# A transformer block's MLP on one core: at the change of layers, three hidden sums are issued ahead of the last additions, and these go from VectorE to GpSimd with their gelus spread over the next products

## The chip, the cores and the metric

The kernel runs on one core of a Trainium2 chip. A core has TensorE (PE, matrix products into PSUM), VectorE (DVE), ScalarE (ACT), GpSimd (POOL) and SyncE (SP, which here only issues DMA transfers). Each engine works through its own queue in order and waits on semaphores that the others raise. The metric is the device time of one execution in microseconds (us). A profiled execution gives the span, from the first to the last instruction.

## The reference

The input x has 2 sequences of 2048 tokens with 512 features, all float32. A condition vector per sequence is turned into shifts, scales and gates. Cut to what matters:

```python
mod = silu(condition) @ Wada + bada
sh_a, sc_a, gt_a, sh_m, sc_m, gt_m = split(mod, 6)
xm = layernorm(x) * (1 + sc_a) + sh_a
x = x + gt_a * attention(xm, Wqkv, Wproj, bproj)      # causal, 16 heads of 32
xm = layernorm(x) * (1 + sc_m) + sh_m
h = gelu(xm @ W1 + b1)                                # 512 -> 2048
x = x + gt_m * (h @ W2 + b2)                          # 2048 -> 512
```

The change touches the last two lines.

## The kernel before, in words

The first two thirds of the span are the projections and the attention of the two sequences; the MLP starts at about 1519 us. It runs over four blocks m = 0 to 3 of 1024 tokens each. In a block, the first layer makes the hidden values h, and the second layer (`tail`) makes the output.

Both layers use Strassen's scheme in Winograd's form: a product of 2x2 blocks is made with seven block products instead of eight, named A11, S1, A12, S2, S3, A22, S4, at the price of sums of blocks of weights and tokens before, and of additions of results after. In blocks 1 to 3 both layers do it on two levels: seven outer products, each of seven inner ones.

*First layer, blocks 1 to 3* (`pair_of_sets`, p = 0 to 3). Pair p makes the hidden features of two columns of 128 in both halves, as four results d00, d01, d10, d11 (d with half and token group), each of two tiles of 128x512. Three phases issue the seven outer products, two or three side by side; `phase` issues in each of seven rounds one inner product of each of its outer products on PE, and behind it the evictions: a copy by ACT (L2162, L2174) or an addition by DVE (`combine`, L1728). Additions between results (`add`, L2221) go to POOL. The last phase makes A22 onto d10 and S3 into t3 (two tiles: in pairs 2 and 3 those of the buffer `Y`, y in the profile's names). Then t3 is added to d11 and to d10, two instructions of 128x512 each. With that the pair's hidden values are whole, and four gelus (L2214, one for each tile of d11 and d10) follow on ACT. In pairs 0 to 2 the additions are POOL's, and the gelus are put on a list (`self.later`) that the next pair's first phase issues after its rounds 3 to 6. In the last pair (`final`) the additions are DVE's, and the four gelus are issued at once, ahead of all of the second layer.

*Second layer* (`tail`). It calls `hid.outer` seven times, in the order A11, S1, A12, S2, S3, A22, S4 of the outer products. Each `outer` calls `seven`, which issues seven products on PE in the order A11, S1, S2, S4, S3, A12, A22 (four matmuls of 128x256 each, which the profile shows as eight instructions) into three PSUM banks a, b and c: A11, S2, S3 and A22 go to a, one on top of the other, S1 and S4 to b, A12 to c. After each, the bank is read before the next product goes on top: in the first outer product, A11, S1 and S2 are copied by ACT into spare tiles (c, L2317), S4, S3 and A12 are combined by DVE into y (L1728), and A22 is copied by ACT into y (L2327).

*Hidden sums* (`Hidden`). The second layer's products need sums of blocks of h. They stand in one list in a fixed order (`todo`): A11's first; the first two of T1 (a difference of whole blocks); S1's first; A11's second, third and fourth; the last two of T1; S1's second to fourth; and so on. A sum (`difference`, L1631) is one instruction of 128x1024. A11's first, T1's first two and S1's first are POOL's, the others DVE's. `pop` issues the next one, if a buffer is free for it. In the last pair's phases the first four are popped, after round 3 of the second phase and after rounds 0, 2 and 4 of the third. In `tail`, `then(k)` pops one after each product k = 0 to 6. `need` is called ahead of a product and pops as many as that product requires: ahead of S1 in the first outer product A11's first and second, ahead of S2 the second and fourth (and so the third).

What else runs beside the tail in blocks 0 to 2: the next block's tokens are loaded (L2452), normalised by ACT (L1622, issued after the fourth product of each of the first four outer products), transposed by PE (ps_xt) after the seventh, and modulated by ACT (L275). The sums for the next block's first layer (L1793, most by POOL) come at the tail's end.

*Order.* The order of each queue is that in which the Python program issues: `act`, `mm` and the helpers around them keep program order. Weights are loaded by SP into four buffers (L1661, L1668); `next_weights` issues the next load when a set has been used. A load waits for its buffer.

Of the kernel before, what the change touches and what calls it, by code (L numbers as in the profile page):

```python
# [27 lines left out]
def dit_block_kernel(  # L28
# [36 lines left out]
    nc = tc.nc  # L65
# [1528 lines left out]
    with ExitStack() as mlp:  # L1594
# [246 lines left out]
        class Hidden:  # L1841
# [3 lines left out]
            def __init__(self):  # L1845
                self.h = [
                    [
                        mp.tile([P, C, MT], F32, tag="h4", name="h4", bufs=2 * FC // C)
                        for _ in range(FC // C)
                    ]  # L1850
                    for _ in range(2)
                ]
                self.todo, self.made, self.at = [], set(), 0
                self.slots, self.later, self.flip = {}, {}, False
                self.t = {n: {} for n in OUTER}
                x = {
                    (g, half): {
                        (j, t): self.h[g][2 * half + j][:, :, t * half_t : (t + 1) * half_t]
                        for j in range(2)
                        for t in range(2)  # L1860
                    }
                    for g in range(2)
                    for half in range(2)
                }
                t1 = {}
                b11, b12, b21, b22 = x[0, 0], x[1, 0], x[0, 1], x[1, 1]
                self.x = {
                    A11: b11, S1: t1, A12: b21, S2: b11, S3: b12, A22: b21, S4: b22,
                }

                def difference_of(name, dst, u, v, after, js=range(2)):
                    for j in js:
                        for t in range(2):
                            self.task(
                                (name, j, t),
                                lambda j=j, t=t: difference(dst[j, t], u[j, t], v[j, t]),
                                after,
                            )

                def first_sums(j):  # L1880
                    for t in range(2):
                        def run(t=t):
                            t1[j, t] = self.take()
                            engine = nc.vector if j else nc.gpsimd
                            difference(t1[j, t], b12[j, t], b11[j, t], engine)
                        self.task(("T1", j, t), run, takes=True)

                def inner(n, ks=(1, 2, 3, 4)):
                    for k in ks:
                        self.task((n, k), lambda k=k: self.inner_sum(n, k), takes=True)  # L1890

                inner(A11, (1,))
                first_sums(0)
                inner(S1, (1,))
                inner(A11, (2, 3, 4))
                first_sums(1)
                inner(S1, (2, 3, 4))
                inner(A12)
                difference_of("T2", b11, b22, t1, 1)
                self.task(("T1", "done"), lambda: self.give(*t1.values()), 2)  # L1900
                inner(S2)
                difference_of("T3", b12, b22, b12, 0)
                inner(S3)
                difference_of("T4", b21, b21, b11, 3)
                inner(A22)
                inner(S4)
# [291 lines left out]
            def pair_of_sets(self, p, among):  # L2198

                final = p == HF // 2 - 1  # L2200
                fs = (2 * p, 2 * p + 1)

                def part(half, g):
                    return [self.part(half, g, f) for f in fs]

                d00, d01, d10, d11 = (part(h, g) for h in range(2) for g in range(2))
                if p < 2:
                    t3 = [self.part(1, 1, f + HF // 2) for f in fs]
                else:
                    t3 = [Y[p][:, j] for j in range(2)]  # L2210

                def gelu(half, d, j):
                    act(
                        nc.scalar.activation(  # L2214
                            d[j], d[j], AF.Gelu, bias=col(r_b1 + half * HF + fs[j], 1)
                        )
                    )

                def add(engine, d, x):
                    for j in range(2):  # L2220
                        act(engine.tensor_tensor(d[j], d[j], x[j], ALU.add))  # L2221

                def phase(ph, jobs):
                    self.flip = not self.flip
                    lanes = []
                    for o, job in enumerate(jobs):
                        if o < 2:
                            banks = bank_pair(self.flip)
                        else:
                            banks = [  # L2230
                                ps_mm.tile(
                                    [P, MT], F32, tag="aa", name=f"ps_{n}", bufs=2
                                )[:, :half_t]
                                for n in "ab"
                            ]
                        n, *to = job
                        lanes.append(self.two_level(n, self.set_of(p * 7 + n), banks, *to))
                    for r in range(7):
                        for lane in lanes:
                            lane[r]()  # L2240
                        among(ph, r)
                        if r in self.later.get(ph, ()):
                            for f in self.later[ph].pop(r):
                                f()
                    for n, *_ in jobs:
                        q = p * 7 + n
                        if q % 2 or q == HF // 2 * 7 - 1:
                            next_weights()
                        if final:
                            sums.append(xi.pop(n))  # L2250
                            k = {S1: 1, S2: 2, S3: 3, A22: 4}.get(n)
                            if k:
                                sums.append(sx.pop(k))

                phase(0, ((S1, d11), (S2, d10), (A11, d00)))
                add(nc.gpsimd, d10, d00)
                add(nc.gpsimd, d11, d10)
                phase(1, ((S4, d01), (A12, d00, d00)))
                add(nc.gpsimd, d01, d11)
                self.later[2] = {  # L2260
                    0: [lambda: gelu(0, d00, 0)], 1: [lambda: gelu(0, d00, 1)],
                    4: [lambda: gelu(0, d01, 0)], 6: [lambda: gelu(0, d01, 1)],
                }
                phase(2, ((A22, d10, d10), (S3, t3)))
                add(nc.vector if final else nc.gpsimd, d11, t3)
                add(nc.vector if final else nc.gpsimd, d10, t3)
                ends = [
                    lambda d=d, j=j: gelu(1, d, j) for d in (d11, d10) for j in range(2)
                ]
                if final:  # L2270
                    for f in ends:
                        f()
                else:
                    self.later[0] = {r: [f] for r, f in enumerate(ends, 3)}

# [69 lines left out]
        def tail(m, hid, among, each):  # L2345

            u, c22, c11, c12 = Y
            later = []

            def gate(y, half):
                later.extend(lambda i=i: gated(m, y, half, i) for i in range(2))

            for n, dst, base in (
                (A11, u, None),  # L2360
                (S1, c22, None),
                (A12, c11, u),
                (S2, u, u),
                (S3, u, u),
                (A22, u, u),
                (S4, c12, c12),
            ):

                def then(k):
                    if k in (1, 3) and later:  # L2370
                        later.pop(0)()
                    hid.pop()
                    among(n, k)

                hid.outer(n, dst, base, then, each if n == S4 else None)
                if n == A12:
                    gate(c11, 0)
                elif n == S2:
                    combine(c12, u, c22)
                elif n == S3:  # L2380
                    combine(c22, c22, u)
                    gate(c22, 1)
                elif n == A22:
                    gate(u, 1)
                elif n == S4 and not each:
                    gate(c12, 0)
            for f in later:
                f()
# [137 lines left out]
```

## Time and profile before

| | |
|---|---|
| median of 3 runs | 2253.81 us (2253.27 to 2258.36) |
| the profiled execution | 2258.55 us, span 2256.8 us |
| PE busy | 2202.7 us, 98% of the span |
| DVE / POOL / ACT busy | 1577.0 / 1429.7 / 1038.1 us |
| the additions L2221 on DVE | 12 in all, four in each of blocks 1, 2 and 3 |
| the four additions in blocks 1, 2 and 3 | start 1787.65, 1970.12 and 2153.51 us, 6.1 us together each time |

A row of the timeline gives the start and the duration in us, the engine, the line, the operation, the tile written, an arrow and the tiles read, the shapes, the number of instructions that the row merges, and in brackets how long the engine sat idle before it and what ended that. PE's ends are modelled, so the time between two products is read from their starts. A row of the windows view gives a stretch, its length, the busy time of PE, PEld (weight loads), DVE, ACT and POOL with the number of instructions, the granted clock of PE (1.00 is full), the share of the DMA engines and GB/s.

### The profile page before, as it was taken

To read this page: it belongs to the slowest core of one execution; us is meant where nothing else is said; L and a number is where in the kernel's file an instruction comes from. 1 tells how busy PE (TensorE), PEld (TensorE's weight loads), DVE (VectorE), ACT (ScalarE), POOL (GpSimd) and SP (SyncE) were. 2 spreads that over 40 slices of the span, in tenths; PEclk is the share of its full clock that TensorE was granted. 3 is DMA by queue.
4 is the path that set the end of the run, shared out by engine and by line. 5 is a ranking of instruction groups with operands and counts; after the bars stand their busy time and mean duration, and the time that the engine had idled before them with its cause. 6 is when DMAs were issued, how large, how long until landed. Compare 5 with 4: busy or idle time off the path is not lost.

```text
span 2256.8 us, 34324 instructions
## 1 busy us (share of the span) xinstructions
PE 2202.7 (98%) x12273; PEld 1475.6 (65%) x12273; DVE 1577.0 (70%) x3385; ACT 1038.1 (46%) x2132; POOL 1429.7 (63%) x891
## 2 busy tenths in 40 slices
PE   7999999999999999999999999999999999999998
PEld 5887555555543588755555555345788888888887
DVE  4678767777757667777677766664686686677576
ACT  4434555655564243355656556513324423532510
POOL 4253998998983695299989898448417516605520
PEclk9999999999999999999999999999999999999999
DMA  8787142231324799533324123367656455554543
GB/s 271 247 277 192 43 93 70 62 85 48 107 95 147 241 308 312 157 77 74 73 75 95 48 60 133 107 228 262 212 167 213 146 178 180 189 163 159 191 149 108
DMA packets 166627, 340.99 MB, mean 151 GB/s; under 512 B 17216, under 2 KB 49516, under 8 KB 164664
## 3 DMA queue, kind: packets, MB, share of 16 engines
q1 hardware_dynamic: 158080, 302.05, 44.0%
q0 software_dynamic: 8000, 36.21, 4.3%
q8 instruction: 97, 1.59, 0.3%
q14 instruction: 74, 0.61, 0.1%
q10 hardware_dynamic: 376, 0.55, 0.1%
HBM read 246.46 MB, written 100.14 MB: 154 GB/s over the span
## 4 chain that ended last, share of the span: by engine, by line
PE 87%; DVE 6%; POOL 3%; DMA 2%; ACT 1%; issue 1%; SPq 0%; DVEq 0%; ACTq 0%; POOLq 0%
PE ps_a L207 23%; PE st L207 18%; PE ps_b L207 13%; PE o L207 10%; PE s L207 9%; PE ps_c L207 4%; PE sm L207 3%; PE ps_o L207 2%; DVE junk L499 1%; POOL ee L696 1%; PE ps_xt L215 1%; ACT e L671 1%; DVE mx L505 1%; DVE h L2221 1%; PE ps_o L215 1%
## 5 line engine op out<-in xcount | busy, mean ns | idle before, releaser
L671 ACT ACTIVATE e<-st 128x512 f32<-128x512 f32 (+1 forms) x1152 | 574.8, 578 | 362.4 <-PE st L207 313.6
L505 DVE TENSOR_REDUCE mx<-s 128x1 f32<-128x512 f32 x576 | 381.8, 686 | 193.8 <-PE s L207 192.8
L696 POOL TENSOR_TENSOR ee<-ee,e 128x2048 f32<-128x2048 f32 x106 | 485.9, 4584 | 10.3 <-ACT e L671 4.4
L207 PE MATMUL st<-qst,kst 128*128 128x512 f32 (+3 forms) x1280 | 408.6, 386 | 0.0
L207 PE MATMUL s<-kst,qst 128*128 128x512 f32 (+3 forms) x1046 | 380.6, 395 | 5.7 <-DVE mx L505 3.7
L207 PE MATMUL ps_a<-sum,w 128*128 128x256 f32 (+1 forms) x1304 | 340.9, 396 | 12.3 <-DVE sum L1631 11.7
L207 PE MATMUL o<-e,vv 128*32 128x512 f32 (+3 forms) x2560 | 293.2, 537 | 0.3 <-POOL e L683 0.3
L207 PEld LDWEIGHTS st<-qst,kst 128*128 128x128 f32 x1280 | 228.5, 188 | 97.7 <-issue 65.9
L207 PEld LDWEIGHTS ps_a<-sum,w 128*128 128x128 f32 x1304 | 249.2, 193 | 55.3 <-ACT c L2317 12.8
L499 DVE CUSTOM_DVE_ANT_0 junk<-s,causal 128x128 bf16<-128x128 f32 (+3 forms) x470 | 220.7, 470 | 61.0 <-PE s L207 47.0
L207 PEld LDWEIGHTS s<-kst,qst 128*128 128x128 f32 x1046 | 194.8, 188 | 70.7 <-DVE mx L505 17.0
L696 POOL TENSOR_TENSOR ee<-e 128x2048 f32<-128x2048 f32 x42 | 192.5, 4584 | 42.6 <-ACT e L671 42.6
L207 PE MATMUL ps_b<-sum,w 128*128 128x256 f32 (+1 forms) x744 | 186.5, 381 | 0.0
L2221 POOL TENSOR_TENSOR h<-h,h 128x512 f32<-128x512 f32 x96 | 119.3, 1273 | 69.6 <-DVE h L1728 69.6
L207 PEld LDWEIGHTS <-sel 32*128 32x128 bf16 x1152 | 29.5, 91 | 197.0 <-issue 196.1
L207 PEld LDWEIGHTS ps_b<-sum,w 128*128 128x128 f32 x744 | 140.7, 190 | 21.7 <-issue 2.6
L1793 POOL TENSOR_TENSOR sum<-xm 128x256 f32<-128x256 f32 x22 | 23.1, 1052 | 185.4 <-PE ps_a L207 185.4
L505 DVE TENSOR_REDUCE mx<-st 128x1 f32<-128x512 f32 x192 | 131.1, 683 | 0.5
L683 POOL TENSOR_SCALAR_AFFINE_SELECT e<-e 128x512 f32<-128x512 f32 x128 | 83.3, 669 | 67.4 <-ACT e L671 67.3
L207 PEld LDWEIGHTS o<-e,vv 128*32 128x32 f32 x2560 | 59.1, 108 | 92.4 <-issue 73.3
L207 PE MATMUL st<-fold,sel 32*128 32x512 bf16 (+1 forms) x1152 | 117.5, 372 | 1.3
L1067 POOL TENSOR_TENSOR lo<-lo,hi 128x512 fp32r<-128x512 f32 x32 | 40.6, 1275 | 104.4 <-ACT hi L1065 99.4
(264 smaller groups left out, 3549.9 us busy)
## 6 DMA issues: line engine op xcount, KB each, us to landing
w<-w1x SPq DMA_DIRECT2D x42, 896.0 KB
qst<-q SPq DMA_DIRECT2D x128, 256.0 KB
kst<-k SPq DMA_DIRECT2D x128, 256.0 KB
w<-w2d SPq DMA_DIRECT2D x28, 1024.0 KB
w<-w2d SPq DMA_DIRECT2D x28, 768.0 KB
q<-hi SPq DMA_DIRECT2D x32, 256.0 KB
q<-lo SPq DMA_DIRECT2D x32, 256.0 KB
k<-hi SPq DMA_DIRECT2D x32, 256.0 KB
```

Source lines behind the costliest of these rows:

```text
L207: return tc.keep_in_program_order(nc.tensor.matmul(*args, **kw))
L215: return tc.keep_in_program_order(nc.tensor.transpose(dst, src, ident[:n, :n]))
L499: nc.vector.tensor_tensor_reduce(junk[:, :w], x, causal[:, QB - w :], 1.0, MASKED, ALU.add, ALU.max, m,)
L505: self.vector(nc.vector.tensor_reduce(m, x, axis=AX.X, op=ALU.max))
L671: act(nc.scalar.activation(e4[:, h, :w], sts[h][:, :w], AF.Exp))
L683: nc.gpsimd.affine_select(d, d, pattern=[[0, HC], [1, P]], compare_op=ALU.is_ge, fill=0.0, base=0, channel_multiplier=-1,)
L696: act(nc.gpsimd.tensor_tensor(dst, x, y, ALU.add))
L1067: engine.tensor_tensor(lo, d, hi.bitcast(F32), ALU.subtract)
L1793: act(engine.tensor_tensor(dst, u, v, ALU.subtract))
L2221: act(engine.tensor_tensor(d[j], d[j], x[j], ALU.add))
```

## The change

In the last pair of blocks 1 to 3, after the last phase: `need` issues A11's second, third and fourth hidden sum at once, on DVE. Then the additions follow, now on POOL and for d10 before d11. The four gelus are put on a new list, `self.ends`, in the order d10, d11. `then` takes one of them after each of the products k = 4, 5, 6 of the first outer product and after product 0 of the second. While that list is not empty, the pops after products 0 and 1 of the first outer product are left out. In pairs 0 to 2 the additions and gelus of d10 also come before those of d11 now.

```diff
@@ Hidden.__init__
                 self.slots, self.later, self.flip = {}, {}, False
+                self.ends = []
@@ pair_of_sets
                 phase(2, ((A22, d10, d10), (S3, t3)))
-                add(nc.vector if final else nc.gpsimd, d11, t3)
-                add(nc.vector if final else nc.gpsimd, d10, t3)
+                if final:
+                    self.need(*[(A11, n) for n in (2, 3, 4)])
+                add(nc.gpsimd, d10, t3)
+                add(nc.gpsimd, d11, t3)
                 ends = [
-                    lambda d=d, j=j: gelu(1, d, j) for d in (d11, d10) for j in range(2)
+                    lambda d=d, j=j: gelu(1, d, j) for d in (d10, d11) for j in range(2)
                 ]
                 if final:
-                    for f in ends:
-                        f()
+                    self.ends = ends
                 else:
                     self.later[0] = {r: [f] for r, f in enumerate(ends, 3)}
@@ tail
                 def then(k):
                     if k in (1, 3) and later:
                         later.pop(0)()
-                    hid.pop()
+                    if hid.ends and (n != A11 or k >= 4):
+                        hid.ends.pop(0)()
+                    if n != A11 or k > 1 or not hid.ends:
+                        hid.pop()
                     among(n, k)
```

## The prediction

> **What bounds the kernel now.** I read the page first, then who waits for whom on TensorE over the part in which the change of layers occurs, then the engines' timelines there, then the granted clock in stretches of 3.41 us. From the page:
>
> ```profile
> PE 2202.7 (98%) x12273; PEld 1475.6 (65%) x12273; DVE 1577.0 (70%) x3385; ACT 1038.1 (46%) x2132; POOL 1429.7 (63%) x891
> ```
>
> PE is busy for 98% of the span, so only what makes PE idle or slow can count. The waits of PE from 1787 us to the end (total, times, longest):
>
> ```profile
> PE ps_a L207 <- DVE sum L1631: 11.7, 3, 3.9
> ```
>
> PE waits for a DVE sum (line 1631) three times, 11.7 us in all, once at each change of layers in blocks 1, 2 and 3. PE's timeline at the first of them, each row one product of the outer seven (eight instructions):
>
> ```profile
> start us, us, engine line op out<-in xcount [idle before <-releaser]
> ...
> 1787.54 1.89 PE L207 MATMUL ps_a<-h,w 128*128 128x256 f32 x8
> 1789.27 1.89 PE L207 MATMUL ps_b<-sum,w 128*128 128x256 f32 x8
> 1795.04 3.62 PE L207 MATMUL ps_a<-sum,w 128*128 128x256 f32 x8 [3.88 <-DVE sum L1631]
> ...
> 1800.23 1.89 PE L207 MATMUL ps_a<-sum,w 128*128 128x256 f32 x8
> ...
> 1803.68 1.89 PE L207 MATMUL ps_a<-sum,w 128*128 128x256 f32 x8
> ```
>
> Products follow each other every 1.73 us (1789.27 - 1787.54). The third product, S2, was due at 1791.00 and starts at 1795.04: 4.04 us of stall. Then S2 and S4 take 5.19 us (1795.04 to 1800.23) where two products take 3.45 (1800.23 to 1803.68): 1.74 us more. At the other two changes:
>
> ```profile
> 1971.74 1.89 PE L207 MATMUL ps_b<-sum,w 128*128 128x256 f32 x8
> 1977.53 3.75 PE L207 MATMUL ps_a<-sum,w 128*128 128x256 f32 x8 [3.90 <-DVE sum L1631]
> ...
> 1983.62 1.89 PE L207 MATMUL ps_a<-sum,w 128*128 128x256 f32 x8
> ...
> 2155.13 1.89 PE L207 MATMUL ps_b<-sum,w 128*128 128x256 f32 x8
> 2160.91 3.75 PE L207 MATMUL ps_a<-sum,w 128*128 128x256 f32 x8 [3.89 <-DVE sum L1631]
> ...
> 2167.47 1.89 PE L207 MATMUL ps_a<-sum,w 128*128 128x256 f32 x8
> ```
>
> The stalls are 4.06 (1977.53 - 1971.74 - 1.73) and 4.05 us, and S2 with S4 take 6.09 and 6.56 us, which is 2.64 and 3.11 over 3.45. So the three changes cost 12.15 us of stall and 7.49 us of slow products, **19.64 us** together. That is the most that the change can win.
>
> Why products run slow stands in the granted clock (column PEclk), in stretches of 3.41 us laid on its switching points:
>
> ```profile
> core 0: us, PE busy (x) PEld busy (x) DVE busy (x) ACT busy (x) POOL busy (x), PEclk, DMA share, GB/s
> 1791.57:1794.98 3.41, 0.00 (x0) 0.00 (x0) 3.41 (x5) 2.39 (x5) 0.43 (x1) 1.00 0.09 33
> 1794.98:1798.40 3.42, 3.36 (x8) 2.76 (x9) 3.32 (x3) 0.08 (x1) 0.00 (x0) 0.50 0.00 0
> 1972.48:1975.89 3.41, 1.15 (x6) 0.67 (x4) 3.41 (x3) 1.38 (x3) 2.01 (x1) 1.00 0.54 199
> ...
> 2160.21:2163.62 3.41, 2.71 (x7) 2.20 (x8) 3.41 (x4) 0.72 (x3) 0.00 (x0) 0.50 0.00 0
> 774.40:777.81 3.41, 1.66 (x8) 1.48 (x9) 1.44 (x5) 1.23 (x4) 0.00 (x0) 1.00 0.79 238
> 777.81:781.22 3.41, 3.41 (x18) 3.00 (x17) 1.87 (x4) 1.00 (x2) 0.30 (x1) 1.00 0.77 245
> ```
>
> The clock falls to half at the end of a stretch in which PE was busy for 0.00, or for 1.15 of 3.41 us; it did not fall after one with 1.66. It stays at half through a stretch with 3.36 us busy and is then full; after 2.71 us busy it was not (the 3.11 above).
>
> **The sum that is late.** GpSimd (POOL) and DVE at the first change, in order of start:
>
> ```profile
> 1786.88 2.38 POOL L1631 TENSOR_TENSOR sum<-h,h 128x1024 f32<-128x1024 f32 x1
> 1787.65 2.15 DVE L2221 TENSOR_TENSOR h<-h,y 128x512 f32<-128x512 f32 x1
> 1789.33 2.67 POOL L1631 TENSOR_TENSOR sum<-sum,sum 128x1024 f32<-128x1024 f32 x1
> 1789.73 2.83 DVE L2221 TENSOR_TENSOR h<-h,y 128x512 f32<-128x512 f32 x1
> ```
>
> and, over the whole run, minimum, median and maximum in ns of these additions on POOL and on DVE:
>
> ```profile
> L2221 POOL TENSOR_TENSOR h<-h,y x12: 1264/1272/1280, 1766.3 to 2135.8; 128x512 f32<-128x512 f32 x12
> L2221 DVE TENSOR_TENSOR h<-h,y x12: 678/1417/2832, 1787.6 to 2158.9; 128x512 f32<-128x512 f32 x12
> ```
>
> The first DVE addition d11 += t3 begins at 1787.65 and takes 2.15 us, the second 2.83, though the same instruction takes 0.68 at its shortest (678 ns). Each ends 0.55 us after the POOL sum beside it (1786.88 + 2.38 = 1789.26, then 1789.33 + 2.67 = 1792.00): two instructions that read two operands in SBUF do not run side by side on DVE and POOL; the later one waits for the whole other. After the four additions come the hidden sums:
>
> ```profile
> 1793.68 1.21 DVE L1631 TENSOR_TENSOR sum<-h,sum 128x1024 f32<-128x1024 f32 x1
> ...
> 1800.50 0.42 DVE L1728 TENSOR_TENSOR y<-c,ps_b 128x256 f32<-128x256 f32 x1 [2.20 <-ACT xn L1622]
> 1800.84 1.22 DVE L1631 TENSOR_TENSOR sum<-h,h 128x1024 f32<-128x1024 f32 x1
> ```
>
> The first of them, A11's second, ends at 1794.89, and PE starts 0.15 us later. On ACT the gelus and the copy that S2 also needs:
>
> ```profile
> 1792.59 1.95 ACT L2214 ACTIVATE h<-h,cols 128x512 f32<-128x512 f32 x3 [2.03 <-DVE h L2221]
> 1794.44 0.35 ACT L2317 COPY c<-ps_a 128x256 f32<-128x256 f32 x1
> ...
> 1798.70 0.37 ACT L2317 COPY c<-ps_a 128x256 f32<-128x256 f32 x1 [3.64 <-PE ps_a L207]
> ...
> 1805.61 0.37 ACT L2327 COPY y<-ps_a 128x256 f32<-128x256 f32 x1 [5.12 <-PE ps_a L207]
> 1806.05 1.93 ACT L275 ACTIVATE xm<-ps_xt,c,a 128x256 f32<-128x256 f32 x4
> ```
>
> The copy of A11's result (1794.44) stood behind four gelus which waited for the additions. So two things hold S2, and the change removes both.
>
> **The change, part by part.**
> *Sums ahead.* A11's sums 2, 3 and 4 are issued on DVE ahead of everything else; the two later calls of the queue that would have issued the first two are left out, so DVE's order after them stays: T1's third sum, the combine of S4, T1's fourth, the combine of S3. No instruction is added. S2's copy waits for no gelu then.
> *Additions to GpSimd.* Four of 128x512 leave DVE and stand on POOL behind its sum S1.1. Alone each takes 1.27 us there. The cover that makes them free would be POOL's own queue, empty after them; but they share the port with the DVE sums. How turns are taken is shown later in the same block, where both queues are full:
>
> ```profile
> 1875.96 1.59 POOL L1793 TENSOR_TENSOR sum<-sum,sum 128x256 f32<-128x256 f32 x1
> 1877.25 1.38 DVE L1631 TENSOR_TENSOR sum<-xm,sum 128x1024 f32<-128x1024 f32 x1
> 1877.51 1.71 POOL L1793 TENSOR_TENSOR sum<-sum 128x256 f32<-128x256 f32 x1
> ```
>
> POOL ends at 1877.55, DVE's sum ends 1.08 later (1878.63), and POOL's next, issued at 1877.51 ahead of that release, ends 0.59 after DVE (1879.22), against 0.73 alone in the row here:
>
> ```profile
> L1793 POOL TENSOR_TENSOR sum<-sum x22: 721/730/1710, 1530.0 to 2074.9; 128x256 f32<-128x256 f32 x22
> ```
>
> So turns alternate, and a waiting instruction has 0.14 us of its time behind it: a DVE sum costs 1.08, an addition on POOL 1.27 - 0.14 = 1.13, S1.1 2.20 (1792.00 less the end of the first addition, 1789.80). DVE's combines read PSUM and run through (0.42, pitch 0.34).
> *The sum at the first change*, each end from the one before: POOL ends T1's second sum 1789.26; A11.2 on DVE 1790.34; S1.1 1792.54; A11.3 1793.62; addition 1794.75; A11.4 1795.83; addition 1796.96; T1's third 1798.04; addition 1799.17 with S4's combine inside it; T1's fourth 1800.25; S3's combine 1800.59. The products: S2 is due at 1791.00 with its sum at 1790.34, no wait; S3 at 1794.46 with 1793.62, no wait; A22 at 1797.92. A22 accumulates in the bank that S3's combine must have read, so it starts at 1800.59 + 0.15 = 1800.74. **A stall of 2.82 us remains, three products later than the old one.** Late next is S3's combine on DVE, behind five sums, each of which waited for a POOL instruction.
> *The clock.* The 2.82 us fall in the stretch 1798.40 to 1801.81 (the old grid) with 1.07 us busy, less than the 1.15 that halved the clock; the next stretch is at half and costs 1.71. Carried on with the shortened time, the grid cuts the second and third stalls so that one stretch holds nearly all of each: 1.71 each. The grid's place differs between executions: where its boundary falls near the middle of the stall the price is 0, where it falls late in it up to 3.1 (row 2160.21).
> *Gelus.* Four of 0.65 us (1.95 for three) move behind products 5, 6, 7 and the next outer product's first. Cover: ACT idles 3.64 and 5.12 us before the rows 1798.70 and 1805.61; the additions that they wait for end at 1794.75 to 1801.4. Behind them on ACT wait A22's copy (1802.6 at the earliest) and the next outer product's copies. Cost nothing; their first reader is a sum of the third outer product, popped in the second. If that cover goes, see the last rival. In pairs 0 to 2 only the order of d10 and d11 is swapped, on POOL and on ACT alike: as many instructions in the same rounds, nothing.
> *Queues.* No DMA moves: the weight loads on SP are issued by products and phases as before. POOL's sums for the next block stand far behind (1875.96). Added waits: POOL's additions wait only for combines done at 1787.7.
> *Sum.* Before 19.64; after 3 x (2.82 + 1.71) = 13.59; gain **6.05 us**. Bounds of the parts: clock 0 to 3.1 at each change, so 8.5 to 17.8 after and a gain of 11.2 to 1.9; without the port, 0 after and 19.6.
> The sum is made on the profiled execution, 2258.55 us (span 2256.8), giving 2252.5. The runs' median is 2253.81, 4.74 lower, so I forecast 2253.81 - 6.05 = **2247.8**.
>
> **Rivals.**
> 1. *The remaining stall is too short for the clock.* Only the stalls stay: 3 x 2.82 = 8.5, gain 11.2, 2242.6. For it: two stretches may share the stall (about a quarter of grid positions). Against it: the stretch with 1.15 us busy. The Trainium skill, TensorE: Matmul & The Clock Gate, section "What's actually happening", says that the clock goes cold after at least one idle window of about 3.4 us; by that rule a gap of 2.82 us would never halve it and the time would be this rival's. The trace agrees only in the window's length: the row 1972.48 was not idle and halved the clock.
> 2. *The port costs nothing at the end*, because POOL gets its turns only in DVE's gaps: S3's combine is then in time, all 19.6 us go, 2234.2. For: DVE idles 2.2 us before 1800.50. Against: POOL was let in at 1877.55 + 1.08 while DVE was full.
> 3. *No net change:* POOL goes twice running. A11.3 then waits for all four additions (1792.54 + 4 x 1.27 + 1.08 = 1798.7), S3 stalls 4.2 us and cold products follow (S3 to 1802.3, A12 to 1804.0 once the clock is back); A22 starts near 1804, as before (1803.68). 2253 to 2254. Against: the alternation shown.
> 4. *Slower: ACT's order.* In the sum d11's first addition ends at 1799.17, and its gelu (0.65) stands ahead of the four modulations (1.93) and the copy (0.37) that the next outer product's S2 needs, due at 1800.74 + 3 x 1.73 = 1805.9 or later. If DVE won every turn, the additions would drag on; from an end of 1803.0 (1805.9 - 2.95) PE waits, and from 1805.0 on the gain of 2.0 per change is gone. At 1807 it is 4.0 of stall and 1.7 of clock less 2.0: +3.7 each, 2265. For: ACT is in order and already stood behind these gelus. Against: POOL got its turn each time.
>
> **How the numbers follow.** Forecast as summed, own range a gain of 2.5 to 9: 0.67, of which 0.30 is over 0.3% (6.8 us, about what a measurement here can tell from no change) because my 6.05 lies just below it. Rival 1: 0.13; rival 2: 0.07; rival 3: 0.05; rival 4: 0.08. Faster 0.30 + 0.13 + 0.07 = 0.50; same 0.37 + 0.05 = 0.42; slower 0.08. The likeliest time lies in "same", though "faster" holds more, since both rivals that gain more add to it. Range: down past rival 1 to 2241, up to 2255 for rival 3 with the spread of the runs; left out are rivals 2 and 4, 0.15.
>
> **What would show it.** PE's wait for a DVE sum at S2 gone; a wait of PE at A22 of about 2.8 us on a DVE combine into y, three times; DVE sums beside POOL additions of about 2.2 us in place of 1.21, and POOL's h<-h,y near 2.2; half clock for about 3.4 us after each; ACT copies of S2's block at about 1789.5. Wrong it would be if PE has no wait there, if A22 starts after 1803.7, or if PE waits in the next outer product.

## The result and the profile after

The changed kernel takes 2249.04 us (median of 10 runs, 2246.31 to 2253.28), the kernel before 2255.89 us over its 10 runs (2253.27 to 2260.64). The ratio is 0.9971, with a 95% interval of 0.9962 to 0.9981: faster by 0.29%. The interval excludes a ratio of 1, but the gain is no larger than the spread of each kernel's own runs: the slowest run of the changed kernel (2253.28) just meets the fastest of the kernel before. The profiled execution took 2248.50 us, span 2246.8.

TensorE's waits from 1760 us on (total, times, longest) no longer name a DVE sum. In its place:

```profile
PE ps_a L207 <- DVE y L1728: 7.8, 3, 2.6
```

The kernel before had 11.7 us in three waits of 3.9 us on a sum; now there are three of 2.6 us on a write of y, the combine (L1728). TensorE's timeline at the first change, one row for each product:

```profile
1787.02 1.89 PE L207 MATMUL ps_b<-sum,w 128*128 128x256 f32 x8
1788.75 1.89 PE L207 MATMUL ps_a<-sum,w 128*128 128x256 f32 x8
...
1793.93 1.89 PE L207 MATMUL ps_c<-h,w 128*128 128x256 f32 x8
1798.40 1.99 PE L207 MATMUL ps_a<-sum,w 128*128 128x256 f32 x8 [2.58 <-DVE y L1728]
1800.23 1.04 PE L215 MATMUL ps_xt<-ident,xn 128*128 128x128 f32 x8
```

S2 (1788.75) follows S1 (1787.02) after 1.73 us, so the old stall is gone. A22 starts 4.47 us after A12 (1793.93), a stall of 2.74 us. DVE there, which issues A11's second to fourth sum, T1's third, S4's combine, T1's fourth and S3's combine, in this order:

```profile
1785.40 2.69 DVE L1631 TENSOR_TENSOR sum<-h,sum 128x1024 f32<-128x1024 f32 x1
1788.01 3.37 DVE L1631 TENSOR_TENSOR sum<-h,h 128x1024 f32<-128x1024 f32 x1
1791.31 2.30 DVE L1631 TENSOR_TENSOR sum<-h,sum 128x1024 f32<-128x1024 f32 x1
1793.53 2.29 DVE L1631 TENSOR_TENSOR sum<-h,h 128x1024 f32<-128x1024 f32 x1
1795.73 0.41 DVE L1728 TENSOR_TENSOR y<-c,ps_b 128x256 f32<-128x256 f32 x1
1796.07 1.95 DVE L1631 TENSOR_TENSOR sum<-h,h 128x1024 f32<-128x1024 f32 x1
1797.94 0.41 DVE L1728 TENSOR_TENSOR y<-c,ps_a 128x256 f32<-128x256 f32 x1
```

and POOL (T1's second sum, S1's first sum, the four additions, now on line 2222):

```profile
1784.64 2.36 POOL L1631 TENSOR_TENSOR sum<-h,h 128x1024 f32<-128x1024 f32 x1
1787.09 3.21 POOL L1631 TENSOR_TENSOR sum<-sum,sum 128x1024 f32<-128x1024 f32 x1
1790.26 8.88 POOL L2222 TENSOR_TENSOR h<-h,y 128x512 f32<-128x512 f32 x4
```

Each DVE sum takes 1.95 to 3.37 us where 1.21 is its time alone. The four additions take 8.88 us, 2.2 each, for 1.27 alone. S3's combine, the row of 1797.94, ends at 1798.35 and A22 starts 0.05 us later. On ACT the copy of A11's result now comes at once (S1's likewise, at 1788.95), and a gelu that waits for POOL holds up nothing that PE needs:

```profile
1787.22 0.37 ACT L2319 COPY c<-ps_a 128x256 f32<-128x256 f32 x1 [0.73 <-PE ps_a L207]
...
1794.76 0.72 ACT L2215 ACTIVATE h<-h,cols 128x512 f32<-128x512 f32 x1 [1.49 <-POOL h L2222]
```

The other two changes:

```profile
1973.47 1.89 PE L207 MATMUL ps_c<-h,w 128*128 128x256 f32 x8
1977.95 3.64 PE L207 MATMUL ps_a<-sum,w 128*128 128x256 f32 x8 [2.59 <-DVE y L1728]
1981.38 1.12 PE L215 MATMUL ps_xt<-ident,xn 128*128 128x128 f32 x8
...
2154.70 1.89 PE L207 MATMUL ps_c<-h,w 128*128 128x256 f32 x8
2159.17 5.32 PE L207 MATMUL ps_a<-sum,w 128*128 128x256 f32 x16 [2.58 <-DVE y L1728]
2164.33 1.89 PE L207 MATMUL ps_b<-sum,w 128*128 128x256 f32 x8
```

The stalls are 2.75 (1977.95 - 1973.47 - 1.73) and 2.74 us. A22 alone then takes 3.43 us at the second (1977.95 to 1981.38), and A22 with A11 of the next outer product 5.16 us at the third: 1.70 us over 1.73 and 3.46 in both. At the first change A22 takes 1.83, 0.10 over. The granted clock (PEclk), in stretches of 3.41 us that are laid on the points at which it switched in this execution (their grid):

```profile
core 0: us, PE busy (x) PEld busy (x) DVE busy (x) ACT busy (x) POOL busy (x), PEclk, DMA share, GB/s
1793.81:1797.22 3.41, 2.01 (x10) 1.42 (x8) 3.41 (x3) 0.72 (x1) 3.41 (x3) 1.00 0.87 271
1797.22:1800.64 3.42, 2.24 (x12) 1.98 (x13) 3.42 (x5) 0.21 (x1) 1.92 (x1) 1.00 0.33 124
1974.72:1978.13 3.41, 0.82 (x4) 0.40 (x4) 3.41 (x5) 0.31 (x1) 3.41 (x2) 1.00 0.87 325
1978.13:1981.54 3.41, 3.41 (x9) 2.59 (x10) 3.41 (x4) 0.00 (x0) 0.55 (x1) 0.50 0.01 5
```

At the first change the boundary at 1797.22 cut the stall, so that the two stretches held 2.01 and 2.24 us of PE's work, and the clock stayed full. At the second, one stretch held 0.82 us and the next ran at half.

The three changes now cost 8.23 us of stall and 3.50 of slow products, 11.73 together against 19.64: 7.91 us less. The spans differ by 10.0 us. The rest lies ahead of anything that the change touches. The MLP's first matmul, before and after:

```profile
1519.05 1.88 PE L207 MATMUL ps_a<-xm,w 128*128 128x512 f32 x4
```

```profile
1516.81 1.88 PE L207 MATMUL ps_a<-xm,w 128*128 128x512 f32 x4
```

From there to the end of the span, the kernel before takes 737.75 us (2256.8 - 1519.05) and the changed one 729.99: 7.76 us less. The other 2.24 us are the difference of the two executions up to the MLP. Over the nine profiles of this study the MLP starts between 1513.1 and 1521.8 us, although no instruction ahead of it differs (the last section says what the traces show of that). So the experiments are compared by the time from this matmul to the end as well, read in the same way:

| kernel | from the MLP's first matmul to the end, us | median, us | ratio to before (95%) |
|---|---|---|---|
| before | 737.75 | 2255.89 | |
| changed | 729.99 | 2249.04 | 0.9971 (0.9962 to 0.9981) |
| T1's last sums later | 721.45 | 2239.76 | 0.9923 (0.9911 to 0.9935) |
| additions on DVE, behind the sums | 728.66 | 2249.05 | 0.9961 (0.9949 to 0.9973) |
| no sums ahead | 729.75 | 2247.27 | 0.9968 (0.9955 to 0.9980) |
| gelus at once | 756.08 | 2275.36 | 1.0081 (1.0067 to 1.0095) |
| before, gelus spread | 737.29 | 2256.17 | 0.9999 (0.9990 to 1.0008) |
| no additions | 718.16 | 2236.36 | 0.9917 (0.9897 to 0.9937) |
| T1's last sums later, made up | 718.50 | 2239.25 | 0.9922 (0.9909 to 0.9935) |

### The profile page after: what moved, and what is told of

It reads as the page before. It is cut to its first block, busy times and chain, and to the rows that moved or that the text cites. A ratio compares the mean times of both kernels' runs of the same rounds, so it can differ in the third digit from the quotient of the medians.

```text
span 2246.8 us, 34306 instructions
## 1 busy us (share of the span) xinstructions
PE 2199.1 (98%) x12273; PEld 1472.7 (66%) x12273; DVE 1581.7 (70%) x3373; ACT 1038.2 (46%) x2132; POOL 1457.1 (65%) x903
## 4 chain that ended last, share of the span: by engine, by line
PE 87%; DVE 6%; POOL 2%; DMA 2%; ACT 1%; issue 1%; SPq 0%; DVEq 0%; ACTq 0%; POOLq 0%
PE ps_a L207 23%; PE st L207 19%; PE ps_b L207 13%; PE o L207 10%; PE s L207 9%; PE ps_c L207 4%; PE ps_o L207 4%; PE sm L207 3%; DVE sum L1631 2%; DVE junk L499 1%; PE ps_xt L215 1%; POOL ee L696 1%; DVE mx L505 1%; ACT e L671 1%; PE ps_o L215 1%
## 5 line engine op out<-in xcount | busy, mean ns | idle before, releaser
L696 POOL TENSOR_TENSOR ee<-ee,e 128x2048 f32<-128x2048 f32 x106 | 485.8, 4583 | 10.3 <-ACT e L671 4.3
```

Source lines behind the costliest of these rows:

```text
L696: act(nc.gpsimd.tensor_tensor(dst, x, y, ALU.add))
```

## The experiments

The theory to be tested has three parts. S2 was held by two things, DVE's additions ahead of the sum and ACT's gelus ahead of the copy. The new stall is S3's combine, late on DVE behind T1's two sums. These are late because DVE and POOL take turns instruction by instruction. The rivals are that the sums ahead alone did it, that POOL's additions simply freed DVE, and that A22 waits for its own sum.

### T1's last two sums later

In the changed kernel, the pops after products 2 and 3 of the first outer product are left out too, so T1's last two sums come behind S3's and A12's combines:

```diff
-                    if n != A11 or k > 1 or not hid.ends:
+                    if n != A11 or k > 3 or not hid.ends:
                         hid.pop()
```

> T1's last two sums are issued behind S3's and A12's combines in place of ahead of them. Theory (A22 waits for S3's combine, which stands on DVE behind these two sums): the 2.74 us wait of PE at A22 goes at all three changes, and with it the half clock behind it; 8.2 us of stall and about 3 of clock less than the changed kernel, near 2238 us. Rival (A22 waits for A11's fourth sum, so for the port as a whole): that sum's place does not change, the wait stays over 2 us and the time at 2249. A second rival: the two sums come too late for the next outer product, and PE waits there instead.

TensorE at the first change (S3, A12, A22), and S3's combine on DVE with T1's third sum behind it:

```profile
1790.74 1.89 PE L207 MATMUL ps_a<-sum,w 128*128 128x256 f32 x8
1792.47 1.89 PE L207 MATMUL ps_c<-h,w 128*128 128x256 f32 x8
1794.19 1.89 PE L207 MATMUL ps_a<-sum,w 128*128 128x256 f32 x8
```

```profile
1792.67 0.42 DVE L1728 TENSOR_TENSOR y<-c,ps_a 128x256 f32<-128x256 f32 x1 [0.20 <-PE ps_a L207]
1793.01 1.34 DVE L1631 TENSOR_TENSOR sum<-h,h 128x1024 f32<-128x1024 f32 x1
```

The combine runs as soon as S3 has ended (1792.67), and A22 follows A12 after 1.72 us. No stall is left at any of the three changes, and the mean granted clock of the profiled execution is 0.999 (0.997 in the changed kernel's). The time falls by another 9 us in the medians and by 8.5 from the MLP's start. The theory holds, and A11's fourth sum was not what A22 waited for. The second rival came true in a small way and at another place: the list now runs two sums late, and in the sixth outer product (A22) PE waits for a sum at S2,

```profile
1849.59 1.99 PE L207 MATMUL ps_b<-sum,w 128*128 128x256 f32 x8
1852.72 1.99 PE L207 MATMUL ps_a<-sum,w 128*128 128x256 f32 x8 [1.14 <-DVE sum L1631]
```

and at two more places like it, 2.9 us in all. These waits account for about the rest of the 11 us that were expected.

### The additions on DVE again, behind the sums

```diff
-                add(nc.gpsimd, d10, t3)
-                add(nc.gpsimd, d11, t3)
+                add(nc.vector if final else nc.gpsimd, d10, t3)
+                add(nc.vector if final else nc.gpsimd, d11, t3)
```

> The changed kernel with its four additions on DVE again, behind A11's three sums. Theory (an addition on POOL takes a turn of 1.13 us at the port, and costs DVE that; on DVE it takes 0.60 of pitch): S3's combine comes about 0.4 us earlier, stall 2.3 in place of 2.74, time 2246 to 2249. Rival (moving the additions frees DVE of 4 x 0.68 us): the stall grows by 2.7 us to 5.4 at each change, and with the clock the time is about 2260.

DVE at the first change (the four additions, T1's third sum, S4's combine, T1's fourth, S3's combine), and TensorE's waits:

```profile
1790.47 2.49 DVE L2222 TENSOR_TENSOR h<-h,y 128x512 f32<-128x512 f32 x4
1792.88 1.21 DVE L1631 TENSOR_TENSOR sum<-h,h 128x1024 f32<-128x1024 f32 x1
1794.01 0.41 DVE L1728 TENSOR_TENSOR y<-c,ps_b 128x256 f32<-128x256 f32 x1
1794.34 1.21 DVE L1631 TENSOR_TENSOR sum<-h,h 128x1024 f32<-128x1024 f32 x1
1795.48 0.41 DVE L1728 TENSOR_TENSOR y<-c,ps_a 128x256 f32<-128x256 f32 x1
```

```profile
PE ps_a L207 <- DVE y L1728: 6.3, 3, 2.1
```

The four additions take 2.41 us in DVE's queue (1790.47 to 1792.88), and the sums around them have 1.21 again. On POOL three of the four additions took a turn each ahead of S3's combine: A11's fourth sum and T1's two sums took 2.30, 2.29 and 1.95 us there. The stall is 2.26 us, 0.48 shorter than with POOL, and the time is the changed kernel's within the intervals. So giving the additions to POOL freed DVE of nothing that counts here. What counts is that they no longer stand ahead of A11's second sum.

### Without the sums ahead

```diff
-                if final:
-                    self.need(*[(A11, n) for n in (2, 3, 4)])
@@ tail
-                    if n != A11 or k > 1 or not hid.ends:
-                        hid.pop()
+                    hid.pop()
```

> The changed kernel without the call that issues A11's three sums ahead, and with all pops as before; the additions stay on POOL and the gelus stay spread. Theory (with no addition on DVE, nothing stands ahead of the sums on DVE either way): the same order on DVE, 2249 within 2 us. Rival (issuing the sums ahead is what takes the wait at S2 away): the wait at S2 comes back, near 2256.

Every engine gets the same instructions in the same order as in the changed kernel, but for the line numbers (DVE's rows in the two profiles agree one by one from the MLP's start), since nothing of DVE's stands between the call and the later pops once the additions are POOL's. TensorE waits for S3's combine as before, three times and 7.7 us in all, and the time is the same (729.75 and 729.99 us). The "sums ahead" of this change are a part without effect of its own. With the additions on DVE, as in the experiment above, their order would matter.

### The gelus at once

```diff
-                    self.ends = ends
+                    for f in ends:
+                        f()
```

(The two pops stay left out in blocks 1 to 3.)

> The changed kernel with its four gelus issued at once, ahead of the first product's copy on ACT. Theory (ACT is in order, and the additions on POOL end 13.4 us after S1's product of the first outer product starts, less 1.7): S2 waits for the copies behind the gelus, a stall of about 11.5 us at each change, 3 x (11.5 - 2.7) = 26 us more than the changed kernel, and the clock as in the kernel before: 2275 to 2282. Rival (ACT's order does not matter, since DVE is the limit): 2249.

The copy of A11's result on ACT at the first change, and TensorE's waits:

```profile
1801.09 0.35 ACT L2320 COPY c<-ps_a 128x256 f32<-128x256 f32 x1
```

```profile
PE ps_a L207 <- ACT c L2320: 30.8, 3, 10.3
```

The copy of A11's result waits until 1801.09 for gelus that wait for POOL, and PE waits up to 10.3 us for it at each change, about a microsecond less than expected. It is slower than the kernel before by 0.8%. With the additions on POOL, spreading the gelus is the part without which the change loses. This does not test the hold that the gelus had in the kernel before: there the copy came at 1794.44, and here the gelus wait for POOL's later additions.

### The kernel before, with its gelus spread

```diff
@@ Hidden.__init__
+                self.ends = []
@@ pair_of_sets
                 if final:
-                    for f in ends:
-                        f()
+                    self.ends = ends
@@ tail
+                    if hid.ends and (n != A11 or k >= 4):
+                        hid.ends.pop(0)()
                     hid.pop()
```

> The kernel before, with its four gelus spread over the products as in the change, d11's first; the additions stay on DVE ahead of the sums. Theory (two things held S2, the copy until 1794.8 us and the sum until 1794.9, so taking the copy's wait alone leaves the other): S2 starts as late as before, a DVE wait of 3.9 us, time within 1.5 us of the kernel before. Rival (the gelus ahead of the copy were the cause): near 2249.

TensorE's waits, and ACT's copy of A11's result:

```profile
PE ps_a L207 <- DVE sum L1631: 11.7, 3, 3.9
```

```profile
1788.72 0.37 ACT L2317 COPY c<-ps_a 128x256 f32<-128x256 f32 x1 [0.73 <-PE ps_a L207]
```

The copy waits for nothing but the product (1788.72; it was 1794.44 before), and the wait for the sum is what it was. The time does not change. So the gelus ahead of the copy were not the only hold: with that wait gone, the sum holds S2 as long as before. That the copy by itself would have held S2 is read from the trace of the kernel before, where it ends at 1794.79 (1794.44 + 0.35), 0.10 us ahead of the sum; no run here takes away the sum's hold alone.

### No additions

```diff
-                add(nc.gpsimd, d10, t3)
-                add(nc.gpsimd, d11, t3)
+                if not final:
+                    add(nc.gpsimd, d10, t3)
+                    add(nc.gpsimd, d11, t3)
```

> The changed kernel without the four additions of the last pair, on any engine: t3 is not added to d10 and d11 there, so half of the last pair's hidden values lack one of their summands. Theory (S3's combine is late because the additions take four turns at the port): without them it ends about 9.9 us after the first product's start, where A22 is due at 10.35: stall gone or under 0.2 us, and the time near 2238. Rival (S1.1 and the five sums on DVE alone make it late): a stall of 1 us or more stays, 2243 or more.

DVE at the first change (T1's third sum, and S3's combine), and A12 and A22 on TensorE:

```profile
1788.77 1.21 DVE L1631 TENSOR_TENSOR sum<-h,h 128x1024 f32<-128x1024 f32 x1
...
1791.37 0.41 DVE L1728 TENSOR_TENSOR y<-c,ps_a 128x256 f32<-128x256 f32 x1
```

```profile
1790.26 1.89 PE L207 MATMUL ps_c<-h,w 128*128 128x256 f32 x8
1791.99 1.89 PE L207 MATMUL ps_a<-sum,w 128*128 128x256 f32 x8
```

The sums behind S1.1 are back at 1.21, S3's combine ends at 1791.78, and A22 starts 1.73 after A12. There is no stall. Without the additions nothing else makes S3's combine late enough to hold PE, and S1.1, which still holds up A11's third sum, does not reach PE by itself. So the additions as a whole make the stall. Taking turns is the smaller part of it: done in DVE's own queue, the additions left a stall of 2.26 us of the 2.74. What S1.1's 2.2 us add while the additions are there was not tested.

### T1's last sums later, and the list made up

The first experiment's kernel with two more pops where DVE idles:

```diff
                     if n != A11 or k > 3 or not hid.ends:
                         hid.pop()
+                    if m and n == S1 and k in (1, 2):
+                        hid.pop()
```

> The variant with T1's last two sums later, and two more calls of the hidden list after products 1 and 2 of the second outer product, where DVE idles 1.8 us: the list stands again where the changed kernel has it. Theory (the 2.9 us of waits that the variant has at 1852.7, 2030.6 and 2204.3 us come from the list's lag of two): they go, about 2237. Rival (they come from the sums' own length there): they stay, 2240.

All of TensorE's waits from 1760 us on, which the kernel before has too (there ACT's line is 2339):

```profile
PE ps_o L215 <- ACT y L2341: 1.5, 1, 1.5
PE ps_o L215 <- DVE xr L1728: 1.1, 3, 0.5
PE ps_a L207 <- DVE c L1728: 0.4, 2, 0.2
```

No wait on a sum is left. From the MLP's start to the end it takes 718.50 us, 2.95 less than the first experiment and 19.25 less than the kernel before, so nearly all of the 19.64. The medians of this kernel and of the first experiment, 2239.25 and 2239.76, do not tell the two apart. The 2.95 us rest on one profile of each, in which the waits at these places are there and are gone. This version beats both kernels: 0.9922 (0.9909 to 0.9935).

## Why the prediction was right, and where it was not

*What bounds, and the 19.64 us.* Right: with every wait at the changes gone, 19.25 us were won.

*Two things hold S2.* Right, in part by experiment: gelus spread without moving the additions gain nothing, so the sum holds S2 by itself, and additions moved without spreading the gelus lose. That the copy held S2 in the kernel before as well is read from its trace, not tested: the additions on DVE behind the sums, with the gelus at once, were not run.

*Sums ahead.* This step of the change, given as what puts the sums first, does nothing. With the additions on POOL the same order arises without it. The sum did not depend on it, but the account of what acts did.

*Additions on POOL, taking turns.* Right, and to a few hundredths. Counted from the end of T1's second sum (1784.64 + 2.36 = 1787.00), S3's combine was predicted 11.33 us later and ended 11.35 later. The stall was predicted as 2.82 and measured as 2.74 to 2.75; PE followed the combine by 0.05 us, not by the 0.15 that was read at S2. The additions cost DVE more on POOL than on its own queue (stall 2.74 against 2.26). The prediction priced this turn by turn, but did not say that leaving them on DVE, behind the sums, would do as well.

*The clock.* This is the term that was off. It stood in the sum at 1.71 at each change, 5.13 in all; the trace shows 0.10, 1.70 and 1.70, 3.50 in all. The first change fell at the grid position of rival 1, where two stretches share the stall. On the profiled executions the gain was 7.8 us in place of 6.05, and the clock makes nearly all of the difference (1.6).

*The level.* 2247.8 was forecast from a median of three runs, 2253.81. Ten runs put the kernel before at 2255.89, and the difference of the medians at 6.85 us. That the forecast time lies only 1.24 us under the measured 2249.04 is in part luck: its base was 2.08 too low and its gain 0.80 too small, and the two errors partly cancel.

*Rivals.* Rival 1 held at one change of three. Rival 2 fell: its time needs the stall gone, and that took leaving the additions out or issuing T1's sums later. Rival 3 fell: turns alternated at every step. Rival 4 did not occur here, but its mechanism is real: with the gelus ahead of the copies, ACT's order costs 10.3 us a change.

*Queues and gelus.* Priced at nothing, and right: from 1760 us on PE has no DMA wait, and on ACT only the one of 1.5 us that the kernel before has too.

## What to carry to other kernels

Before work is given to another engine, look at whether the instructions of the two run side by side. Here they took turns: an addition of 0.60 us in DVE's own queue became a turn of 1.12 us on POOL in which DVE waited (T1's fourth sum ended 2.20 us after its third, of which 1.08 is the sum). When an in-order engine frees a bank, put that instruction ahead of whatever is needed only later: moving two sums behind a combine was worth 8.5 us here, more than the change itself. And when two waits end within 0.1 us of each other, removing one shows nothing, as the spread gelus did here; remove both before judging either.

## What was not expected of the hardware

The clock of PE halved after stalls well under one stretch of 3.41 us. The prediction had taken this from one row of the kernel before and priced it at every change; how often it comes was not expected. In the three profiles with a remaining stall of 2.26 to 2.75 us (the changed kernel, the additions on DVE, no sums ahead), it halved after 6 of 9 stalls, by where the grid cut them. Two stretches of one profile, that without the sums ahead, come closest to each other, at the first change and at the second, each with the stretch behind it:

```profile
1791.68:1795.10 3.42, 1.38 (x7) 0.87 (x5) 3.42 (x3) 0.72 (x1) 3.42 (x3) 1.00 0.92 322
1795.10:1798.51 3.41, 2.88 (x7) 2.31 (x8) 3.41 (x5) 0.00 (x0) 1.27 (x1) 0.50 0.13 50
1972.59:1976.00 3.41, 1.40 (x7) 0.90 (x5) 3.41 (x3) 0.72 (x1) 3.41 (x3) 1.00 0.93 341
1976.00:1979.42 3.42, 2.86 (x17) 2.61 (x18) 3.42 (x5) 0.83 (x2) 1.29 (x1) 1.00 0.09 33
```

A stretch with 1.38 us of work halved the clock, one with 1.40 did not. The other stretches at full clock in these three profiles and in that of the kernel before agree: those with less work (among them 0.82 and 0.97 us in the changed kernel, 1.15 in the kernel before) halved it, those with more (1.66 in the kernel before, 2.01 in the changed one) did not. So in these runs the line lies near 1.4 of 3.41 us, an estimate from modelled ends of PE's products. The first experiment's three stalls, 0.87 to 1.41 us long, did not halve it. The Trainium skill, TensorE: Matmul & The Clock Gate, section "What's actually happening", has the clock go cold after at least one idle window of about 3.4 us. The length of the window agrees (the row of 1978.13 above is at half for one whole stretch); that the window must be idle does not.

The second thing is the spread of the MLP's start, 8.7 us over nine profiles with the same instructions ahead of it, more than the change is worth. The traces show a part of it, though not what starts it. Around 20 us from the start, the clock is at half for two stretches in the profile whose MLP starts last (1521.8), for one in the kernel before, the changed kernel and the gelus at once, and not in the other five. And PE's idle time up to 1510 us, added up as the profile has it, goes from 31.8 us in the profile whose MLP starts first (1513.1) to 35.0 in the kernel before. Why the idle time differs stays open.
